# Factorization-machine layer on one core: groups of 1536 columns, outer sums by accumulating DMAs, a 4x2x3 scheme for one of seven inner products

## The chip, the cores and the metric

The kernel runs on one core of a Trainium2 chip. The core has a matrix engine (TensorE, here PE, with its weight loads shown apart as PEld), a vector engine (VectorE, DVE), a scalar engine (ScalarE, ACT), a general engine (GpSimd, POOL) and a queue engine (SyncE, SP) that issues most DMAs. Each engine works through its own instructions in their order and waits on semaphores for the others. The metric is the device time of one execution in microseconds; the median of three runs is 1438.88 us before the change (1438.18 to 1439.22).

## What is computed

```python
out_lin = x @ lin_w.T + lin_b
xv = jnp.einsum('bf,efm->bem', x, weight)
zp = jnp.einsum('bf,efm->bem', jnp.square(x), jnp.square(weight))
interaction = 0.5 * jnp.sum(jnp.square(xv) - zp, axis=1)
return out_lin + interaction
```

x is 1024 x 512, weight 64 x 512 x 512 (embedding e, feature f, model column m), all float32. For every m there are 64 columns of weight, so `xv` is a product of 1024 x 512 with 512 x 32768. Since the second term is summed over e before it is used, it needs only the sums over e of the squared weights (`w2_sum`) and one small product.

## The kernel before

The large product is cut into 16 groups of 32 model columns, 2048 columns each. In each group a fast scheme with seven products (of Strassen's kind) is used twice. The outer one splits x into two halves of rows and two halves of features, and the weight group into quadrants `w11`, `w12`, `w21`, `w22`. Its seven right-hand sides are four quadrants, possibly after a sum in place, and `T1`, `T2`; the sums between quadrants are made by `outer_sum` (L384), eight DVE instructions of 128x1024 a group. Its left-hand sides are sums of blocks of x, kept for all groups in `X1` to `X7`.

Each of the seven outer products is made by `tree` (L416), in the order of `ORDER` (1, 6, 2, 7, 4, 5, 3), again with seven products. `tree` forms four sums `t1` to `t4` on POOL (128x512 each), then runs seven products of two matmuls with 512 columns each (L438). A float32 matmul shows as two MATMUL records with a LDWEIGHTS each, so a group has 196 records. Partial results are shared between products in PSUM: ACT copies a bank to SBUF (`p5`, `p53`) or to another bank (`b2`) at L287 while PE accumulates on; DVE adds banks to `p` or to the outer accumulators `oa`, `ob`, `c` (`outer_psum` L451, `outer_sbuf` L465, all issued at L274); POOL does most adds whose operands both lie in SBUF. When a quadrant of the group's result is complete, `finish` (L402) squares it on ACT (L289) and reduces it over e on DVE (L296) into `acc`. `w_squares` (L394) does the same for the weight quadrants, into `w2_sum`.

At the start the linear part is 32 matmuls (L325) whose result goes to DRAM; at the end 32 matmuls (L565) form the product with `w2_sum`, and the accumulators come back from DRAM.

The order is made when the program is built, by the class `Plan`: every operation has a cost per engine, reads and writes, and `Plan.order` (L62) runs a list schedule. On PE the order is fixed by a key (`7 * s + PLACE[p]`): `pick` takes the next product of the chain or none. The other engines take the operation that is due first among those that are ready. Adds whose operands are in SBUF may go to DVE or POOL. What comes out is one fixed sequence for each engine; nothing is chosen on the chip.

Of the kernel before, what the change touches and what calls it, by code (L numbers as in the profile page):

```python
# [17 lines left out]
G = 2  # L18
ORDER = (1, 6, 2, 7, 4, 5, 3)

SLOT = {1: 0, 7: 1, 2: 2, 4: 3, 5: 4, 6: 5, 3: 6}

PLACE = {5: -6, 3: -2, 1: 0, 6: 3, 2: 4, 7: 6, 4: 9}
# [3 lines left out]
class Plan:  # L27

# [14 lines left out]
    def add(self, costs, emit, reads=(), writes=(), key=None, land=0.0, both=False):  # L43
        op = SimpleNamespace(
            n=len(self.ops), costs=costs, emit=emit, key=key, land=land,
            deps=set(), succ=[], latest=None, end=None, both=both,
        )
        for r in reads:
            if r in self.writer:
                op.deps.add(self.writer[r])  # L50
        for w in writes:
            op.deps.update(self.readers[w])
            if w in self.writer:
                op.deps.add(self.writer[w])
# [4 lines left out]
        op.deps.discard(op.n)  # L59
        self.ops.append(op)  # L60

    def order(self, spare=4.0):  # L62
# [6 lines left out]
        for o in reversed(ops):  # L69
            for d in o.deps:  # L70
                ops[d].succ.append(o.n)
        waiting = [len(o.succ) for o in ops]
        stack = [o for o in ops if not o.succ]
        while stack:
# [3 lines left out]
            for x in o.succ:  # L78
                latest = min(latest, ops[x].latest - cost)
# [11 lines left out]
        done, late, nxt = [], 0.0, 0  # L91
# [5 lines left out]
        def ready(o):  # L97
            return max([0.0] + [ops[d].end for d in o.deps]) + self.HOP
# [35 lines left out]
        while len(done) < len(ops):  # L134
            now = heapq.heappop(times)
            moved = True
            while moved:
                moved = False
                for e in pending:
# [6 lines left out]
                    if e == PE:  # L146
                        nxt += 1
# [25 lines left out]

@with_exitstack
def kernel(
# [8 lines left out]

    nc = tc.nc
    NG, NQ, _, NCB, KH, N = weight.shape
    B = xT.shape[1]
    M = out.shape[1]
    NB = B // P
    NK = 2 * KH
    MG = M // NG
    MI = MG // 4  # L210
    E = N // MI
    H = B // 2
    Q = B // 4

# [9 lines left out]

    buf = {}

    def make(name, shape, pool=sb):
        buf[name] = pool.tile(shape, F32, tag=name, name=name)
        return name

    def ring(tag, n, shape, pool=sb):
        names = [make(f"{tag}_{i}", shape, pool) for i in range(n)]
        state = [0]

        def take():
            state[0] += 1
            return names[(state[0] - 1) % n]
# [3 lines left out]
    half = [P, 2, N]  # L241
    for i in range(1, 8):
        make(f"X{i}", [P, 7, Q])
    for q in ("w11", "w12", "w21", "w22a", "w22b", "T1", "T2"):
        for c in range(NCB):
            make(f"{q}.{c}", half)
    for pos in range(4):
        make(f"oa{pos}", half)
        make(f"ob{pos}", half)
    t_ring = {k: ring(f"t{k}", 2, [P, N]) for k in range(1, 5)}  # L250
    p5_ring, p53_ring = ring("p5", 2, half), ring("p53", 3, half)
    c_ring, wsq_ring = ring("c", 3, half), ring("wsq", 2, half)
    make("b1", [P, G, N], ps)
    make("b3", [P, G, N], ps)
    b2_ring = ring("b2", 2, [P, G, N], ps)
    acc_ring = ring("acc", 2, [P, NB, MG])
    w2_sum = sb.tile([P, NK, M], F32, tag="w2_sum", name="w2_sum")
    bias = sb.tile([P, M], F32, tag="bias", name="bias_sb")
# [5 lines left out]
    PAIR = 1.72  # L264

    def two_input(o, a, b, sub, size=1024, psum=False):

        costs = {DVE: 0.08 + 1.06 * size / 1024}
        if not psum:
            costs[POOL] = 0.14 + 2.19 * size / 1024  # L270

        def emit(e):
            f = engines[e].tensor_sub if sub else engines[e].tensor_add
            f(o, a, b)  # L274

        return costs, emit

    def whole(o, a, b, sub=False, only=None, psum=False):

        costs, emit = two_input(buf[o], buf[a], buf[b], sub, psum=psum)  # L280
        plan.add({e: c for e, c in costs.items() if only in (None, e)}, emit, (a, b), (o,),
                 both=not psum)

    def act(o, i, func, reads, writes, cost=1.04):
        def emit(_):
            if func is None:
                nc.scalar.copy(o, i)  # L287
            else:
                nc.scalar.activation(o, i, func)  # L289

        plan.add({ACT: cost}, emit, reads, writes)

    def reduce(o, i, reads, writes):
        plan.add(
            {DVE: 1.14},
            lambda _: nc.vector.tensor_reduce(  # L296
                o, i.rearrange("p a (m e) -> p a m e", e=E), axis=AX.X, op=ALU.add
            ),
            reads, writes,
        )  # L300
# [3 lines left out]


    x_src = xT.rearrange("(p k) b -> p k b", k=NK)
    lw_src = lin_wT.rearrange("(p k) m -> p k m", k=NK)
    nc.gpsimd.dma_start(bias, lin_b.partition_broadcast(P))
    for k in range(NK):
        q, r = divmod(k, KH)  # L310
        for h in range(2):
            name = f"oa{2 * h + q}"
            dma(buf[name][:, r, :], x_src[:, k, ts(h, H)], (), ((name, r),),
                1.2, 2.0, nc.sync if h == 0 else nc.scalar)
        dma(buf[f"ob{q}"][:, r, :], lw_src[:, k, :], (), ((f"ob{q}", r),), 1.2, 2.0)

    lin_banks = ["b1", "b3", "b2_0", "b2_1"]
    for k in range(NK):
        q, r = divmod(k, KH)
        for g, bank in enumerate(lin_banks):  # L320
            h = g // 2

            def emit(_, k=k, q=q, r=r, g=g, h=h, bank=bank):
                for j in range(G):
                    nc.tensor.matmul(  # L325
                        buf[bank][:, j, :],
                        buf[f"oa{2 * h + q}"][:, r, ts((g * G + j) % (NB // 2), P)],
                        buf[f"ob{q}"][:, r, :],
                        start=(k == 0),
                        stop=(k == NK - 1),  # L330
                    )

            plan.add({PE: PAIR}, emit, ((f"oa{2 * h + q}", r), (f"ob{q}", r)),
                     (bank,), key=-1000 + 4 * k + g)
    for g, bank in enumerate(lin_banks):
        o = ("ob2", "ob3", "c_0", "c_1")[g]
        for j in range(G):
            costs, emit = two_input(buf[o][:, j, :], buf[bank][:, j, :], bias, False, 512, True)
            plan.add(costs, emit, (bank,), ((o, j),))
        dma(lin_dram[:, ts(g, G), :], buf[o], ((o, 0), (o, 1)), (o,))  # L340

    def block4(i):
        return buf[f"X{i}"][:, 0:4, :].rearrange("p (k q) b -> p k (q b)", k=2)

    a_buf = {"A11": "oa0", "A12": "oa1", "A21": "oa2", "A22": "oa3"}

    def a_parts(*names):
        return tuple((a_buf[n], r) for n in names if n in a_buf for r in range(KH)) + tuple(
            n for n in names if n not in a_buf
        )  # L350

    def a_ap(n):
        return buf[a_buf[n]] if n in a_buf else block4(int(n[1]))

    for i, n in ((1, "A11"), (2, "A12"), (4, "A22")):
        act(block4(i), a_ap(n), None, a_parts(n), (f"X{i}",))
    for i, a, b, sub in ((5, "A21", "A22", 0), (6, "X5", "A11", 1), (7, "A11", "A21", 1), (3, "A12", "X6", 1)):
        costs, emit = two_input(block4(i), a_ap(a), a_ap(b), sub)
        plan.add(costs, emit, a_parts(a, b), (f"X{i}",), both=True)
    for i in ORDER:  # L360
        x = buf[f"X{i}"]
        a11, a21, a12, a22 = (x[:, s, :] for s in range(4))
        s1, s2, s4 = (x[:, s, :] for s in range(4, 7))
        for o, a, b, sub in ((s1, a21, a22, 0), (s2, s1, a11, 1), (s4, a12, s2, 1), (a21, a11, a21, 1)):
            costs, emit = two_input(o, a, b, sub, 256)
            plan.add(costs, emit, (f"X{i}",), (f"X{i}",), both=True)
    for n in a_buf.values():
        plan.add({SP: 0.0}, None, (), (n,) + tuple((n, r) for r in range(KH)))
    for n in ("ob0", "ob1", "ob2", "ob3", "c_0", "c_1"):
        plan.add({SP: 0.0}, None, (), (n, (n, 0), (n, 1)))  # L370


    QUAD = ("w11", "w12", "w21", "w22")

    def w(g, q):
        return q + "ab"[g % 2] if q == "w22" else q

    def load(g):
        for q in (0, 1, 3, 2):
            for c in range(NCB):  # L380
                n = f"{w(g, QUAD[q])}.{c}"
                dma(buf[n], weight[g, q][:, c], (), (n,))

    def outer_sum(g, which):  # L384
        o, a, b = {
            1: ("T1", "w12", "w11"),
            2: ("T2", w(g, "w22"), "T1"),
            3: ("w12", w(g, "w22"), "w12"),
            4: ("w21", "w21", "T2"),
        }[which]  # L390
        for c in range(NCB):
            whole(f"{o}.{c}", f"{a}.{c}", f"{b}.{c}", True, DVE)

    def w_squares(g, q):  # L394
        row, col = divmod(QUAD.index(q), 2)
        for c in range(NCB):
            n, sq = f"{w(g, q)}.{c}", wsq_ring()
            act(buf[sq], buf[n], AF.Square, (n,), (sq,), 1.07)
            m = g * MG + (2 * col + c) * MI
            reduce(w2_sum[:, ts(row, KH), m:m + MI], buf[sq], (sq,), (("w2", row, m),))  # L400

    def finish(g, i, n, pos):  # L402
# [211 lines left out]
```

## Time and profile before

| | us |
|---|---|
| median of the runs | 1438.88 |
| span of the profiled execution, first to last instruction | 1436.8 |
| PE busy | 1408.8 |
| DVE busy | 1245.7 |
| POOL busy | 1149.6 |
| ACT busy | 748.8 |

The runs' times hold a little more than the span, which begins with the first instruction and ends with the last. Busy times add up an engine's instructions; matmuls are pipelined and their records overlap, so the pitch from one to the next says more than their length. In a group's row stand line, engine, operation, result and operands by the program's names, shape and count, then busy time in us and the mean of one in ns, then the idle time just before it and what ended it. The granted clock of TensorE is 1.000 on average.

### The profile page before, as it was taken

How to read it: one execution, taken by the hardware profiler on the slowest of the kernel's cores; microseconds unless marked ns; L12 is line 12 of the kernel's file. 1: busy time of each engine (PE TensorE's matmuls, PEld its weight loads, DVE VectorE, ACT ScalarE, POOL GpSimd, SP SyncE). 2: the span in 40 equal slices, each digit the busy share in tenths (PEclk: the TensorE clock that was granted, in tenths of full speed). 3: DMA queues.
4: the chain of work that ended last, by engine and by line, in shares of the span. 5: the costliest groups of instructions: out<-in, count | busy, mean ns of one | idle time of the engine just before them, and what ended most of it. 6: DMA issues, size and time to landing. Idle time of an engine off the chain costs nothing.

```text
span 1436.8 us, 10763 instructions
## 1 busy us (share of the span) xinstructions
PE 1408.8 (98%) x3264; PEld 619.3 (43%) x3264; DVE 1245.7 (87%) x1006; ACT 748.8 (52%) x756; POOL 1149.6 (80%) x691
## 2 busy tenths in 40 slices
PE   7999999999999999999999999999999999999998
PEld 3444444444444444444444444444444444444443
DVE  1899898998989899898988989899898888989984
ACT  1465554645545465564556555465554546556441
POOL 6988886878878688896878888687887868889781
PEclk9999999999999999999999999999999999999999
DMA  5311111111111112111111111111111111210221
GB/s 212 117 60 58 48 59 33 59 48 59 59 42 51 33 59 62 46 58 33 59 48 58 59 48 59 33 59 48 58 59 45 53 32 57 60 52 22 88 74 59
DMA packets 40377, 83.54 MB, mean 58 GB/s; under 512 B 18240, under 2 KB 19264, under 8 KB 40320
## 3 DMA queue, kind: packets, MB, share of 16 engines
q1 hardware_dynamic: 39664, 81.54, 18.1%
q10 hardware_dynamic: 576, 1.05, 0.2%
q8 instruction: 27, 0.44, 0.1%
q14 instruction: 30, 0.25, 0.1%
q0 software_dynamic: 80, 0.26, 0.0%
HBM read 76.68 MB, written 6.16 MB: 58 GB/s over the span
## 4 chain that ended last, share of the span: by engine, by line
PE 90%; POOL 4%; DVE 2%; issue 1%; ACT 1%; DMA 1%; DVEq 0%; POOLq 0%; SPq 0%
PE b L438 86%; POOL oa L274 3%; PE b L325 2%; PE b L565 2%; ACT p L287 1%; POOL t L274 1%; DMA ob<-lin_wT 0%; DVE p L274 0%; DMA T1.1_83<-lind 0%; DVE ob L274 0%; DVE w11.1_73 L536 0%; DVE w21.0_76 L274 0%; DVE oa L274 0%; DVE acc L296 0%; DVE w11.0_72 L536 0%
## 5 line engine op out<-in xcount | busy, mean ns | idle before, releaser
L438 PE MATMUL b<-t,X 128*128 128x512 f32 x1792 | 806.2, 592 | 2.0 <-DVE p L274 1.6
L438 PEld LDWEIGHTS b<-t,X 128*128 128x128 f32 x1792 | 340.0, 190 | 431.9 <-issue 415.0
L287 ACT COPY p<-b 128x1024 f32<-128x1024 f32 x224 | 225.6, 1007 | 266.1 <-PE b L438 226.8
L289 ACT ACTIVATE oa<-oa 128x1024 f32<-128x1024 f32 x128 | 131.9, 1054 | 165.3 <-DVE oa L274 90.9
L296 DVE TENSOR_REDUCE w_sum<-wsq 128x16 f32<-128x1024 f32 x128 | 154.8, 1211 | 29.0 <-ACT wsq L289 28.9
L287 ACT COPY b<-b 128x1024 f32<-128x1024 f32 x112 | 111.8, 998 | 91.1 <-PE b L438 85.2
L274 DVE TENSOR_TENSOR p<-b,p 128x1024 f32<-128x1024 f32 x96 | 117.0, 1218 | 43.4 <-PE b L438 43.4
L296 DVE TENSOR_REDUCE acc<-oa 128x16 f32<-128x1024 f32 x128 | 152.0, 1207 | 0.0
L438 PE MATMUL b<-w21.0_76,X 128*128 128x512 f32 x256 | 120.3, 592 | 0.0
L274 POOL TENSOR_TENSOR oa<-oa,p 128x1024 f32<-128x1024 f32 x32 | 102.8, 3212 | 1.8
L289 ACT ACTIVATE c<-c 128x1024 f32<-128x1024 f32 x64 | 67.7, 1058 | 67.8 <-DVE c L274 67.8
L274 POOL TENSOR_TENSOR oa<-p,oa 128x1024 f32<-128x1024 f32 x32 | 75.7, 2365 | 27.2 <-DVE p L274 26.9
L274 DVE TENSOR_TENSOR oa<-b,p 128x1024 f32<-128x1024 f32 x64 | 78.0, 1219 | 11.7 <-PE b L438 10.8
L274 POOL TENSOR_TENSOR c<-c,oa 128x1024 f32<-128x1024 f32 x32 | 75.4, 2357 | 13.8 <-DVE c L274 11.7
L274 POOL TENSOR_TENSOR oa<-oa,ob 128x1024 f32<-128x1024 f32 x32 | 76.4, 2387 | 6.9 <-DVE oa L274 6.9
L274 POOL TENSOR_TENSOR ob<-ob,oa 128x1024 f32<-128x1024 f32 x32 | 76.3, 2384 | 5.5 <-DVE ob L274 5.5
L274 POOL TENSOR_TENSOR t<-w21.0_76,t 128x512 f32<-128x512 f32 x32 | 40.8, 1275 | 48.3 <-PE b L438 48.3
L274 POOL TENSOR_TENSOR ob<-p,ob 128x1024 f32<-128x1024 f32 x32 | 75.7, 2364 | 0.5 <-DVE p L274 0.5
L296 DVE TENSOR_REDUCE acc<-ob 128x16 f32<-128x1024 f32 x64 | 75.9, 1209 | 0.0
L296 DVE TENSOR_REDUCE acc<-c 128x16 f32<-128x1024 f32 x64 | 74.8, 1208 | 1.1 <-ACT c L289 1.1
L438 PEld LDWEIGHTS b<-w21.0_76,X 128*128 128x128 f32 x256 | 48.6, 190 | 61.2 <-issue 61.2
L274 DVE TENSOR_TENSOR ob<-b,oa 128x1024 f32<-128x1024 f32 x32 | 39.1, 1223 | 40.5 <-PE b L438 39.8
(127 smaller groups left out, 2295.9 us busy)
## 6 DMA issues: line engine op xcount, KB each, us to landing
w11.0_72<-weight SPq DMA_DIRECT2D x16, 512.0 KB, 3.7
w11.1_73<-weight SPq DMA_DIRECT2D x16, 512.0 KB, 3.8
w12.0_74<-weight SPq DMA_DIRECT2D x16, 512.0 KB, 3.8
w12.1_75<-weight SPq DMA_DIRECT2D x16, 512.0 KB, 3.8
w21.0_76<-weight SPq DMA_DIRECT2D x16, 512.0 KB, 3.8
w21.1_77<-weight SPq DMA_DIRECT2D x16, 512.0 KB, 4.7
w22a.0_78<-weight SPq DMA_DIRECT2D x8, 512.0 KB, 3.8
w22a.1_79<-weight SPq DMA_DIRECT2D x8, 512.0 KB, 3.8
```

The lines of the kernel that those rows point to most:

```text
L274: f(o, a, b)
L287: nc.scalar.copy(o, i)
L289: nc.scalar.activation(o, i, func)
L296: lambda _: nc.vector.tensor_reduce(o, i.rearrange("p a (m e) -> p a m e", e=E), axis=AX.X, op=ALU.add),
L325: nc.tensor.matmul(buf[bank][:, j, :], buf[f"oa{2 * h + q}"][:, r, ts((g * G + j) % (NB // 2), P)], buf[f"ob{q}"][:, r, :], start=(k == 0) ...
L438: nc.tensor.matmul(buf[b][:, j, :], buf[f"X{i}"][:, SLOT[p], ts(j, P)], op, start=first, stop=True, skip_group_check=True,)
L565: nc.tensor.matmul(buf[bank][:, j, :], buf[xe[h, k // KH]][:, k % KH, ts((g * G + j) % (NB // 2), P)], w2_sum[:, k, :], start=(k == 0), st ...
```

## The change

The groups become two of 16 model columns (1024 columns) and then twenty of 24 (1536 columns). Matmuls have 256 columns in the first two groups and 384 in the others.

`outer_sum` no longer runs on DVE: `T1` and `T2` are loaded from DRAM as copies of `w12` and `w22`, and the four sums of a group are DMAs that add to their destination, issued from POOL's queue. Signs in the x blocks are changed so that all four are additions. `T1` gets a second buffer.

On PE, `Plan.order` takes, among the products that are ready and due within 20 us, the one with the lowest key. Dependencies are kept by regions (`Reg`) of one large tile for each name instead of by tile, and two-row tiles become strided regions. The rings of `p53` and of the sums `t` are shorter.

Outer product 1 of each wide group is made by `wide_tree`: four row blocks by two feature blocks by three column blocks with 20 products of one 256-column matmul each, where `tree` has 14 matmuls of 384. It needs eight sums on POOL, and more PSUM copies on ACT. `widen` turns `X1` into the 20 left-hand sides, once.

```diff
-G = 2
+HK = (1,)
+HSEQ = (17, 10, 0, 19, 7, 4, 6, 3, 14, 16, 9, 1, 18, 11, 12, 8, 2, 15, 5, 13)
+TBUF = 3
+SPARE = 4.0
+AHEAD = 20.0
...
+def groups(n_m):
+    return [16, 16] + [24] * ((n_m - 32) // 24)
...
             if e == PE:
-                if nxt < len(chain):
-                    o = chain[nxt]
-                    if not left[o.n] and ready(o) <= now + 1e-6:
-                        return o
-                return None
+                able = [n for n in pending[e]
+                        if ops[n].latest < now - late + AHEAD and ready(ops[n]) <= now + 1e-6]
+                return ops[min(able, key=lambda n: ops[n].key)] if able else None
...
+    def dma_add(o, i, rows, reads, writes):
+        token = ("token", len(plan.ops))
+
+        def emit(_):
+            nc.gpsimd.dma_start(o, i, accum_op=ALU.add)
+
+        cost = 2.9 * rows / 1024
+        plan.add({POOL: 1.0}, emit, reads + writes, writes + (token,), land=cost + 2.5)
+        plan.add({SP: cost}, None, (token,), ())
...
     def outer_sum(g, which):
-        o, a, b = {
-            1: ("T1", "w12", "w11"),
-            2: ("T2", w(g, "w22"), "T1"),
-            3: ("w12", w(g, "w22"), "w12"),
-            4: ("w21", "w21", "T2"),
-        }[which]
-        for c in range(NCB):
-            whole(f"{o}.{c}", f"{a}.{c}", f"{b}.{c}", True, DVE)
+        o, i = {
+            1: (w(g, "T1"), None), 2: ("T2", w(g, "T1")), 3: ("w12", w(g, "w22")), 4: ("w21", "T2"),
+        }[which]
+        n = KH * GROUPS[g] // 2 * E
+        o = reg(o, 0, n)
+        if i is None:
+            dma_add(o.ap, source(g, 0), n, (), o.atoms)
+        else:
+            dma_add(o.ap, reg(i, 0, n).ap, n, reg(i, 0, n).atoms, o.atoms)
...
+    def wide_tree(time, g, i, fresh_bank):
...
+        sums = (
+            (t(9), bk(0, 1), bk(1, 1), 0),
+            (t(0, 2), cols(0), twice(bk(0, 1)), 1),
+            (t(2, 2), t(0, 2), twice(bk(1, 1)), 1),
+            (t(4, 2), t(2, 2), cols(1), 0),
+            (t(11), bk(1, 0), bk(1, 2), 0),
+            (t(8), t(11), bk(1, 1), 1),
+            (t(6, 2), t(0, 2), twice(t(8)), 0),
+            (t(10), t(6), bk(0, 0), 0),
+        )
+        for o, a, b, sub in sums:
+            tt(o, a, b, sub, POOL)
...
+        def product(p, b, half, first=False):
+            mm([h(b, half)], [reg(f"X{i}", HSLOT[p] * P, P)], rhs[p], first,
+               time + (HSEQ.index(p) - HLEAD) * cost)
...
+        product(17, "U", 0, True)
+        copy(Reg(h("Q").tile, h("Q").off, V, (V, 2)), twice(h("U", 0)))
+        product(10, "T", 1, True)
+        product(0, "T", 0)
+        copy(h("S"), h("T"))
+        copy(pp, h("T"))
...
+        product(13, "S", 0)
+        leave("S", 0, (0, 1), n5, extra_sub=True)
...
+    for g, mg in enumerate(GROUPS):
         acc_name[g] = acc_ring()
-        load(g)
+        load(g, (("w11", 0), ("w12", 1), (w(g, "T1"), 1), ("T2", 3)))
         outer_sum(g, 1)
         outer_sum(g, 2)
+        load(g, ((w(g, "w22"), 3), ("w21", 2)))
...
+            hk = i in HK and mg == max(GROUPS)
+            if hk and GROUPS[g - 1] != mg:
+                widen(i)
```

More of the change, by code (lines that the diff above doesn't have):

```diff
@@ L236, in take @@
             state[0] += 1
-            return names[(state[0] - 1) % n]
+            return names[(state[0] - 1) % len(names)]
         return take
-    half = [P, 2, N]
     for i in range(1, 8):
-        make(f"X{i}", [P, 7, Q])
-    for q in ("w11", "w12", "w21", "w22a", "w22b", "T1", "T2"):
-        for c in range(NCB):
[L246 to L258, printed above, removed]
+        make(f"X{i}", 20 * P if i in HK else 7 * Q)
+    for q in ("w11", "w12", "w21", "w22a", "w22b", "T1a", "T1b", "T2"):
+        make(q, KH * WIDE)
+    make("oa", 4 * WIDE)
+    make("ob", 4 * WIDE)
+    make("c", 4 * WIDE)
+    t_ring = ring([make(f"t{k}", 12 * V) for k in range(TBUF)])
+    p5_ring = ring([make(f"p5_{k}", WIDE) for k in range(2)])
+    p53_ring = ring([make(f"p53_{k}", WIDE) for k in range(2)])
+    wsq_ring = ring([make(f"wsq{k}", WIDE) for k in range(2)])
+    for name in ("b1", "b3", "b2_0", "b2_1"):
+        make(name, 2 * N, ps, N)
+    b2_ring = ring(["b2_0", "b2_1"])
+    acc_ring = ring([make(f"acc{k}", NB * max(GROUPS), sb, 4) for k in range(2)])
+    make("w2_sum", NK * M, sb, 4)
+    make("bias", M)
     acc_dram = dram.tile([P, NB, M], F32, tag="accd", name="accd")
@@ L272, in emit @@
         def emit(e):
             f = engines[e].tensor_sub if sub else engines[e].tensor_add
[L274 to L284, printed above, removed]
+            f(o.ap, a.ap, b.ap)
+        plan.add({e: c for e, c in costs.items() if only in (None, e)}, emit,
+                 a.atoms + b.atoms, o.atoms, both=not psum)
@@ L285, in emit, with copy @@
+    def copy(o, i, negative=False):
         def emit(_):
-            if func is None:
-                nc.scalar.copy(o, i)
-            else:
[L289 to L300, printed above, removed]
+            if negative:
+                nc.scalar.activation(o.ap, i.ap, AF.Copy, scale=-1.0)
+            else:
+                nc.scalar.copy(o.ap, i.ap)
+        plan.add({ACT: 0.19 + 0.00083 * o.size}, emit, i.atoms, o.atoms)
@@ L337 @@
[L337 to L349, printed above, removed]
-        )
@@ L352, in a_ap @@
[L352 to L359, printed above, removed]
+        name, off = ("c", g * 2 * M) if g < 3 else ("w22b", 0)
@@ new lines, with x_block, minus_both @@
+        for j in range(2):
+            tt(reg(name, off + j * M, M), reg(bank, j * N, N), reg("bias"))
+        o = reg(name, off, 2 * M)
+        dma(lin_dram[:, ts(g, 2), :].rearrange("p a m -> p (a m)"), o.ap, o.atoms, (("lin", g),))
+    def x_block(i):
+        return reg(f"X{i}", 0, 4 * Q)
+    for i, a in ((1, (0, 0)), (2, (0, 1)), (4, (1, 1))):
+        copy(x_block(i), x_in(*a))
+    def minus_both(o, a, b):
+        plan.add(
+            {DVE: 0.08 + 1.06 * o.size / 1024},
+            lambda _: nc.vector.scalar_tensor_tensor(
+                o.ap, a.ap, -1.0, b.ap, ALU.mult, ALU.subtract
+            ),
+            a.atoms + b.atoms, o.atoms, both=True,
+        )
@@ L550 @@
[L550 to L555 removed]
+            {DVE: 0.15 + 1.09 * 2 * (hi - lo) / 1024},
+            lambda _: nc.vector.scalar_tensor_tensor(
+                view(r, lo, hi), a, 0.5, view(r, lo, hi), ALU.mult, ALU.add
+            ),
```

508 lines of the change are left out of this document (341 added, 167 removed).

## The prediction

> **What bounds the kernel now.** I read first the busy shares on the page, then the chain of work that ended last in order of time.
>
> ```profile
> span 1436.8 us, 10763 instructions
> PE 1408.8 (98%) x3264; PEld 619.3 (43%) x3264; DVE 1245.7 (87%) x1006; ACT 748.8 (52%) x756; POOL 1149.6 (80%) x691
> ```
> ```profile
> 1.19 6.57 DMA ob<-lin_wT
> 7.90 30.40 PE b L325 x64
> ...
> 1225.26 3.30 POOL oa L274
> 1230.59 79.25 PE b L438 x184
> 1310.46 3.30 POOL oa L274
> ...
> 1404.63 27.48 PE b L565 x64
> ```
>
> PE is the bound: its weight of 98% is no artefact of long records, because the last 64 matmul records (32 matmuls, two records each) follow each other without a gap in 27.48 us, 0.42938 us each. At that pitch 3264 records take 1401.5 us. The other 35.3 us of the span are: 7.9 before the first matmul; 30.40 - 27.48 = 2.9 because the first records ran slower; 4.7 behind the last matmul (1436.8 - 1404.63 - 27.48); and about 20 of waits.
>
> ```profile
> PE b L438 <- ACT p L287: 13.4, 16, 1.1
> ```
>
> A group comes every 85.2 us (1310.46 - 1225.26); its 196 records at 0.42938 need 84.16, so 1.04 us is lost at each group border, 16 times by the list of waits. The timeline there shows how (start, duration, engine, line, operation; in brackets the idle time and its releaser):
>
> ```profile
> 714.02 3.33 POOL L274 TENSOR_TENSOR oa<-oa,p 128x1024 f32<-128x1024 f32 x1
> 717.30 2.25 POOL L274 TENSOR_TENSOR t<-w21.1_77,w21.0_76 128x512 f32<-128x512 f32 x1
> 719.52 1.27 POOL L274 TENSOR_TENSOR t<-w11.0_72,t 128x512 f32<-128x512 f32 x1
> 720.75 1.27 POOL L274 TENSOR_TENSOR t<-T2.1_85,T2.0_84 128x512 f32<-128x512 f32 x1
> 721.98 2.38 POOL L274 TENSOR_TENSOR ob<-p,ob 128x1024 f32<-128x1024 f32 x1
> 724.30 1.29 POOL L274 TENSOR_TENSOR t<-T2.1_85,t 128x512 f32<-128x512 f32 x1
> ```
> ```profile
> 717.38 1.06 ACT L289 ACTIVATE oa<-oa 128x1024 f32<-128x1024 f32 x1 [4.64 <-POOL oa L274]
> 718.34 0.99 ACT L287 COPY p<-b 128x1024 f32<-128x1024 f32 x1
> ```
> ```profile
> 715.06 3.36 DVE L274 TENSOR_TENSOR T2.0_84<-w22a.0_78,T1.0_82 128x1024 f32<-128x1024 f32 x1
> 718.35 1.21 DVE L274 TENSOR_TENSOR p<-b,p 128x1024 f32<-128x1024 f32 x1
> ```
>
> ```profile
> 716.68 1.88 PE L438 MATMUL b<-w22b.0_80,X 128*128 128x512 f32 x4
> 719.39 1.98 PE L438 MATMUL b<-w11.1_73,X 128*128 128x512 f32 x4 [0.82 <-ACT p L287]
> ```
>
> POOL's add takes 3.33 us beside a DVE outer sum that reads two SBUF tiles (3.36), against 2.38 for the same size a few adds later; the next, of 512, takes 2.25 against 1.27. ACT's square waits for that add, ACT's copy of a PSUM bank stands behind the square in ACT's queue, and PE waits for the copy: its four records from 716.68 are over at 718.40, the next start at 719.39. So the border stall is a late POOL, passed on through ACT.
>
> **PE's work after.** From the program's order I count 3360 records of 384 columns, 1192 of 256 and 128 of 512. By columns alone they cost 3360 x 0.32204 + 1192 x 0.21469 + 128 x 0.42938 = 1392.9 us, 8.6 less than before; that is the 20-product scheme (5120 columns a group instead of 5376). Against it stand 1416 more records.
>
> ```profile
> 8.88 0.34 PEld L325 LDWEIGHTS b<-ob,oa 128*128 128x128 f32 x1 [0.52 <-issue]
> ...
> 13.15 0.28 PEld L325 LDWEIGHTS b<-ob,oa 128*128 128x128 f32 x1 [0.52 <-issue]
> 13.67 0.19 PEld L325 LDWEIGHTS b<-ob,oa 128*128 128x128 f32 x1 [0.24 <-issue]
> ```
>
> A fixed part per record can be read from the start, where the same records ran at half speed. Five steps from 8.88 to 13.15 are 0.854 each. If streaming halves exactly and a fixed part is hidden in the slow state, streaming is 0.427 and the fixed part 0.0024. Then the records cost 0.3227, 0.2159 and 0.4294, together 1396.5 us: 5.0 less than before. I take this; its bounds are 1392.9 (no fixed part) and 1400 (twice as much).
>
> ```profile
> 709.61 0.40 PEld L438 LDWEIGHTS b<-w22b.0_80,X 128*128 128x128 f32 x2 [0.46 <-DVE ob L274]
> 710.25 0.19 PEld L438 LDWEIGHTS b<-w22b.0_80,X 128*128 128x128 f32 x1 [0.24 <-issue]
> ```
>
> A 256-column record must still cover the next weight load, 0.19 us; the cover left is 0.026, and two loads have stood back to back in 0.40, so a pitch of 0.20 is possible. If a load did stick out, each 0.01 us would cost 1192 x 0.01 = 12 us.
>
> A wide group so has 168 x 0.3227 + 40 x 0.2159 = 62.8 us of PE. Everything else must fit in that.
>
> **DVE and ACT.** DVE loses its outer sums, 128 + 15 instructions that read two SBUF tiles, and so the partner of POOL's 3.3 us adds; in the built order DVE has no such instruction in the middle groups. A wide group leaves it 50 instructions of 768 elements and 4 of 256.
>
> ```profile
> 1386.08 1.13 DVE c L274
> 1387.21 1.13 DVE acc L296
> ```
> ```profile
> L274 DVE TENSOR_TENSOR p<-b,p 128x1024 f32<-128x1024 f32 x96 | 117.0, 1218 | 43.4 <-PE b L438 43.4
> L274 DVE TENSOR_TENSOR ob<-b,bias_sb 128x512 f32<-128x512 f32 x4 | 2.6, 681 | 12.2 <-PE b L325 12.2
> L289 ACT ACTIVATE c<-c 128x1024 f32<-128x1024 f32 x64 | 67.7, 1058 | 67.8 <-DVE c L274 67.8
> ```
>
> From 1.13 us from start to start at 1024 and the difference to a 512 one, 0.86 at 768 and 0.33 at 256. That is 44.3 of 62.8 us (71%, before 87%). ACT has 51 instructions a group, most of them shorter than before; at the full price of a 1024 one, 1.06, they make 54. Neither becomes the bound.
>
> **POOL is the tight one.** POOL's starts in the border rows are 1.23 apart behind a 512 add and 2.32 behind a 1024 one (721.98 to 724.30): 0.14 + 2.13 ns per element, so 0.685 at 256, 0.958 at 384, 1.775 at 768. A wide group gives it 24 of 384, 14 of 768, 4 of 512, 4 of 256 and four DMA issues: 23.0 + 24.9 + 4.9 + 2.7 = 55.5 us and four issues. Slack is 7.3 us less the issues.
>
> ```profile
> L308 POOL DMA_DIRECT2D bias_sb<-lin_b x1 | 0.7, 677 | 0.8 <-POOLq L603 0.8
> ```
> ```profile
> w11.0_72<-weight SPq DMA_DIRECT2D x16, 512.0 KB, 3.7
> w21.1_77<-weight SPq DMA_DIRECT2D x16, 512.0 KB, 4.7
> bias_sb<-lin_b POOLq DMA_DIRECT2D x1, 256.0 KB, 7.4
> ```
>
> The only DMA on POOL's queue so far is the bias. Its issue took 0.677 us for rows of 2 KB; the new rows are 6 KB. Bounds for one issue: 0.68 and 3 x 0.68 = 2.03; I take 1.0, nearer the lower end since both have 128 rows. POOL then has 59.5 of 62.8 us, 95%, where it had 80% before. From 1.83 us an issue on, POOL and not PE sets the group.
>
> What stands behind the DMAs on POOL matters as much, for POOL goes in order. In the built order the sum into w21 is followed by 2 adds of 768 and 3 of 384 until the first add that reads it (6.4 us of work); T2 by 7.9 us; w12 by 10.2; T1 by 24 instructions. A landing later than that stops all of POOL, and with it ACT's squares and PE as at the border. Bounds for the landing of 768 KB: 3.7 (a 512 KB load, nothing dearer) and 14.1 (4.7 x 1.5 for the bytes, twice because the destination is read too). I take 7, the slow load scaled by its bytes: 0.6 us of waiting a group, inside the slack of 3.3. The Trainium skill, DMA: Bandwidth & Descriptors, section Anatomy of one DMA — SWDGE (gpsimd) path, fits 2.0 us plus bytes at 436 GB/s for a DMA issued from GpSimd, an estimated 3.8 us here; by it POOL never waits, the sum stays and the chance of the slower rival below goes to the forecast. No run here shows an accumulating DMA, and the page does not say that its fit holds for one.
>
> ```profile
> q1 hardware_dynamic: 39664, 81.54, 18.1%
> ```
>
> SP, whose queue carries the loads, issues 12 a group instead of 8. The DMA engines were 18% busy and get, counting an accumulation double, 14 quarter passes over the weights for 4, so at most 63%. Loads are a group ahead, so I cost them at nothing; without that cover they lengthen the landing, which is in its range.
>
> **Stalls after.** The 16.7 us at the borders (16 times 1.04) rest on a locked POOL add; that goes.
>
> ```profile
> 1357.62 5.42 PE L438 MATMUL b<-t,X 128*128 128x512 f32 x12 [0.37 <-POOL t L274]
> 1394.14 3.67 PE L438 MATMUL b<-t,X 128*128 128x512 f32 x8 [0.20 <-DVE p L274]
> 1402.68 1.96 PE L438 MATMUL b<-t,X 128*128 128x512 f32 x4 [1.44 <-DVE p L274]
> ```
>
> The waits near the end (0.37, 0.20 and 1.44 us) I leave as they are in kind, about 2 us.
>
> New ones: taking matmuls as they become ready only changes a fixed order, on the chip PE still stops at the first one that is not; a POOL at 95% leaves perhaps 0.2 us a wide group, 4 us, bounds 0 and 1.04.
>
> ```profile
> 11.76 1.52 POOL L274 TENSOR_TENSOR X<-X 128x256 f32<-128x256 f32 x2 [9.84 <-ACT X L287]
> ```
>
> At the start POOL gets all 28 sums of 256 on X (25 before): 19.2 us, with 4.6 for two whole blocks, 19.2 and 17.2 for the first group's adds and 4 for its issues, 64 us. POOL can begin at 11.7 and is done at 76, PE with the first narrow group at 7.9 + 30.4 + 196 x 0.2159 = 80.6: hidden, by 5 us. The widening of X1 is 12 short adds on POOL, about 6 us in all, spread up to the second narrow group; if they find no slack they cost 6 us once.
>
> Sum: 1396.5 + 7.9 + 2.9 + 4.7 + 2 + 4 = 1418 span. Executions run about 2 us over the span (median 1438.88 against 1436.8), so **1420 us**.
>
> **The rivals.**
> - No new stall at all and no fixed part: 1392.9 + 15.5 + 2.1 = 1410. For it: DVE's relief; against it: POOL's 95%.
> - The stall only moves. The 4x2x3 tree has longer chains of PSUM copies with half-bank products; if PE loses 1.04 us in each of 20 groups, 1396.5 + 15.5 + 2 + 20.8 + 2 = 1437, the same as before. Here the change would not do what it says. For it: the border stalls passed through ACT, whose queue is as in-order as ever; against it: the order puts neighbouring trees' products between the tree's steps.
> - POOL's issue is dear: at 2.03 us POOL has 63.6 a group, 0.8 over PE: 16 us more than forecast less the 4 already in, 1432. For: three times the bytes; against: the same number of rows.
> - Slower: accumulating DMAs land late and POOL stands in front of the first reader. A landing of L costs (L - 6.4) + (L - 7.9) a group, less 3.3 of slack, 20 times; it eats the forecast's 19 us from L = 9.3 on, and at L = 10 it is 48 us: 1468. For: the 7.4 us of the bias with a third of the bytes, though it ran beside the first loads; against: 3.7 for plain loads.
>
> **How the numbers follow.** Chances: forecast 0.55, none lost 0.08, stall moves 0.09, dear issue 0.10, late landing 0.18. A difference within 0.2% (2.9 us, about what a measurement of this kernel can tell from none) counts as the same. Faster are the forecast, the case without stalls, the dear issue and 0.04 of the moved stall, together 0.77; the other 0.05 of the moved stall is the same; the late landing is slower, 0.18. The range reaches from 1409, just under the case without stalls, to 1446, some way into the late landings: about 0.15 is left above and 0.02 below it. The forecast's own range is 1411 to 1430.
>
> **What would show it.** In the profile after: 384-column records 0.32 apart and 256 ones 0.216 (right) or more (the load sticks out); no add on POOL longer than 1.9 us at 768; POOL busy near 90 to 95%; POOL idle less than 2 us a group in front of reads of w21, T2 or w12 (right) or more than 4 (the slower rival); groups 62.8 to 63.2 us apart. Wrong would be groups of 64 us and more.

## The result and the profile after

The changed kernel takes 1485.08 us (median of three runs, 1483.65 to 1488.68) against 1438.88: ratio 1.0327, 95% interval 1.0313 to 1.0341. It is slower; the forecast of 1420 and its range up to 1446 missed. The profiled execution's own time is 1488.68 us.

The busy shares of the page after:

```profile
span 1486.9 us, 15088 instructions
PE 1425.1 (96%) x4680; PEld 883.4 (59%) x4680; DVE 1058.4 (71%) x1255; ACT 806.8 (54%) x1158; POOL 1296.5 (87%) x1139
```

PE fell from 98 to 96%, and no other engine took its place. What PE's work itself costs is seen in its timeline (start, duration, operation, count):

```profile
50.61 1.89 PE L335 MATMUL b<-t,X 128*128 128x256 f32 x8
52.34 1.89 PE L335 MATMUL b<-T,X 128*128 128x256 f32 x8
...
736.63 1.45 PE L335 MATMUL b<-T,X 128*128 128x384 f32 x4
737.92 1.45 PE L335 MATMUL b<-t,X 128*128 128x384 f32 x4
```

Eight records of 256 columns take 1.73 us, 0.216 each; four of 384 take 1.29, 0.3225 each. At 0.2159, 0.3226 and 0.4294 us for records of 256, 384 and 512 columns the 4680 records cost 1396.3 us. The time that was lost is between the records. The chain of waits shows one wide group and the next:

```profile
689.85 42.52 PE b L335 x134
...
732.45 0.58 ACT b L299
...
733.07 8.90 PE b L335 x34
...
742.00 0.70 DVE oa L289
...
742.78 0.38 ACT oa L299
...
743.18 0.44 DVE oa L289
...
743.64 0.78 ACT b L299
744.42 1.00 ACT p L299 x2
...
745.47 52.04 PE b L335 x164
...
798.21 8.90 PE b L335 x34
...
810.60 19.54 PE b L335 x61
```

The same place returns after 810.60 - 745.47 = 65.13 us, where PE has 62.8 us of work: 2.3 us are lost in each wide group. They are lost at two places, both inside `wide_tree`, and the list of PE's waits puts them down to ACT's copies of PSUM banks, once each in 19 groups; the wait for `c` and several for `oa` belong to the start:

```profile
PE b L335 <- ACT p L299: 16.9, 19, 0.9
PE b L335 <- ACT b L299: 13.6, 19, 0.7
PE b L335 <- DVE c L289: 7.0, 1, 7.0
PE b L335 <- DVE oa L289: 6.7, 8, 3.4
```

`wide_tree` calls the six PSUM banks that it uses Q to V; a bank is 512 float32 columns of PSUM, the memory that matmuls write to. The first stall stands in front of product 7, which writes bank Q; the copy it waits for writes bank S from T. Product 7 touches neither S nor T. The second stands in front of product 5, again in Q; it waits for the copy `n5` out of S, and that copy (the second of the two in the last row below; the row's shape is the first one's) stands in ACT's queue behind copies for other trees, one of which waits for DVE. Here is that queue, and an add of DVE beside it:

```profile
742.78 0.37 ACT L299 COPY oa<-b 128x256 f32<-128x256 f32 x1 [2.57 <-DVE oa L289]
743.64 0.78 ACT L299 COPY b<-b 128x768 f32<-128x768 f32 x1 [0.49 <-DVE oa L289]
744.34 1.08 ACT L299 COPY p<-b 128x768 f32<-128x768 f32 x2
```
```profile
742.00 0.69 DVE L289 TENSOR_TENSOR oa<-b,p 128x512 f32<-128x512 f32 x1 [0.98 <-PE b L335]
```

Q and S are two banks of one tile (`b2_0` or `b2_1`, two banks each). The planner of the changed kernel counts what touches a tile by bank (`make(name, 2 * N, ps, N)`). In the built program the wait goes by tile, so far as these rows tell: an instruction on one bank waits for the last one on the other bank too. The first row of ACT shows it where both only read: that copy reads V, and it waits 2.57 us until DVE's add, which reads R, is over; R and V are two banks of one tile. So the planner put product 7 right behind the copy, thinking that it was free to run. Before the change the planner counted by whole tiles too, and the two countings agreed. The runs below test this.

The gaps can be added up over the whole trace: from the start of one matmul record to the next, less 0.2159, 0.3226 or 0.4294 by its columns (records at half clock count with their excess). That gives 34.0 us from 0 to 300 us, 37.8 from 300 to 1340 (16 groups of 2.3) and 7.3 after; before the change it was 7.3, 12.5 and 2.7. The start is the second loss, though not all of another kind: the first wide group begins before 145 us, and its tree's stalls and those of the next are in the 34.0. DVE and POOL there:

```profile
34.12 7.74 DVE L391 SCALAR_TENSOR_TENSOR X<-oa,X 128x1024 f32<-128x1024 f32 x1
41.78 2.47 DVE L289 TENSOR_TENSOR c<-b,bias 128x512 f32<-128x512 f32 x4
```
```profile
34.34 1.03 POOL L289 TENSOR_TENSOR X<-X 128x256 f32<-128x256 f32 x1
35.02 1.02 POOL L289 TENSOR_TENSOR t<-w 128x256 f32<-128x256 f32 x1
...
39.80 0.97 POOL L289 TENSOR_TENSOR t<-w,t 128x256 f32<-128x256 f32 x1
41.94 0.73 POOL L289 TENSOR_TENSOR X<-X 128x256 f32<-128x256 f32 x1 [1.17 <-DVE X L391]
```
```profile
43.20 2.04 PE L335 MATMUL b<-t,X 128*128 128x256 f32 x4 [7.03 <-DVE c L289]
```

`minus_both`, with two SBUF inputs on DVE, lasts 7.74 us: POOL's adds go on beside it at 0.68 us from start to start, and it ends 1.1 us after the last of them is over (40.77 to 41.86). The bias adds of the linear part stand behind it in DVE's queue, and PE waits 7.03 us for their banks.

### The profile page after: what moved, and what is told of

Read it like the earlier page. It is cut to its first block, busy times and chain, and to the rows that moved or that the text cites. A ratio compares the mean times of both kernels' runs of the same rounds, so it can differ in the third digit from the quotient of the medians.

```text
span 1486.9 us, 15088 instructions
## 1 busy us (share of the span) xinstructions
PE 1425.1 (96%) x4680; PEld 883.4 (59%) x4680; DVE 1058.4 (71%) x1255; ACT 806.8 (54%) x1158; POOL 1296.5 (87%) x1139
## 4 chain that ended last, share of the span: by engine, by line
PE 87%; ACT 4%; DVE 3%; DMA 2%; issue 1%; POOL 0%; DVEq 0%; ACTq 0%; SPq 0%
PE b L335 86%; DVE oa L289 2%; ACT b L299 2%; PE b L776 2%; ACT p L299 1%; DMA w<-weight 1%; DMA w<-T 1%; DVE acc L314 0%; ACT oa L299 0%; DVE p L289 0%; DMA T1b<-lind 0%; DMA X<-xT 0%; DVE X L744 0%; DVE T1b L758 0%; ACT wsq L305 0%
## 5 line engine op out<-in xcount | busy, mean ns | idle before, releaser
L335 PE MATMUL b<-t,X 128*128 128x384 f32 (+1 forms) x2584 | 832.1, 464 | 45.3 <-ACT p L299 16.2
L335 PEld LDWEIGHTS b<-t,X 128*128 128x128 f32 x2584 | 484.0, 191 | 347.5 <-ACT p L299 28.3
L335 PE MATMUL b<-w,X 128*128 128x384 f32 (+1 forms) x1176 | 369.1, 447 | 4.9 <-DVE oa L289 4.2
L299 ACT COPY p<-b 128x768 f32<-128x768 f32 (+1 forms) x328 | 230.3, 714 | 215.6 <-PE b L335 215.3
L335 PEld LDWEIGHTS b<-w,X 128*128 128x128 f32 x1176 | 224.5, 191 | 123.6 <-ACT p L299 5.7
L289 POOL TENSOR_TENSOR t<-w 128x384 f32<-128x384 f32 (+2 forms) x196 | 198.1, 1028 | 78.4 <-PE b L335 65.5
L305 ACT ACTIVATE oa<-oa 128x768 f32<-128x768 f32 (+1 forms) x176 | 142.5, 822 | 177.3 <-DVE oa L289 135.8
L314 DVE TENSOR_REDUCE w_sum<-wsq 128x12 f32<-128x768 f32 (+1 forms) x176 | 160.5, 923 | 66.1 <-ACT wsq L305 65.9
L314 DVE TENSOR_REDUCE acc<-oa 128x12 f32<-128x768 f32 (+1 forms) x176 | 157.3, 921 | 9.6 <-ACT oa L305 9.5
L289 POOL TENSOR_TENSOR t<-w,t 128x384 f32<-128x384 f32 (+1 forms) x136 | 138.8, 1021 | 4.3 <-PE b L335 2.9
```

What stands on the lines that cost most here:

```text
L289: f(o.ap, a.ap, b.ap)
L299: nc.scalar.copy(o.ap, i.ap)
L305: lambda _: nc.scalar.activation(o.ap, i.ap, AF.Square), i.atoms, o.atoms)
L314: nc.vector.tensor_reduce(o, x, axis=AX.X, op=ALU.add)
L335: nc.tensor.matmul(a.ap, b.ap, w.ap, start=start, stop=True, skip_group_check=True)
```

## The experiments

All medians are beside runs of the kernel before on the same chip (1438.4 to 1438.7; 1438.9 for the first row). "Group" is the mean time from one wide group to the next, "gaps" are PE's as above, from 0 to 300 and from 300 to 1340 us. Both are read from one profiled execution, which for e5 and e10 was the fastest of ten (1438.9 and 1432.1 us).

| kernel | median, us | ratio to before (95%) | group, us | gaps 0-300 | gaps 300-1340 |
|---|---|---|---|---|---|
| after | 1485.1 | 1.0327 (1.0313-1.0341) | 65.1 | 34.0 | 37.8 |
| e1_no_wide | 1458.8 | 1.0140 (1.0125-1.0155) | 64.1 | 22.1 | 15.0 |
| e2_tile_deps | 1497.0 | 1.0412 (1.0396-1.0427) | 66.0 | 29.5 | 49.3 |
| e3_split_two | 1508.0 | 1.0487 (1.0471-1.0502) | 66.3 | 37.3 | 53.9 |
| e4_split_one | 1429.1 | 0.9940 (0.9923-0.9957) | 62.9 | 16.9 | 1.3 |
| e5_start | 1443.2 | 1.0029 (1.0020-1.0039) | 62.9 | 27.1 | 1.2 |
| e6_one_no_wide | 1434.2 | 0.9970 (0.9958-0.9982) | 63.2 | 15.6 | 0 |
| e7_dve_sums | 1514.7 | 1.0530 (1.0496-1.0564) | 67.3 | 28.1 | 69.2 |
| e8_strict | 1585.5 | 1.1017 (1.0999-1.1036) | 70.4 | 43.0 | 111.3 |
| e9_pool_only | 1440.7 | 1.0015 (1.0004-1.0026) | 63.5 | 17.9 | 11.1 |
| e10_pool_adds | 1435.2 | 0.9974 (0.9965-0.9984) | 63.4 | 12.0 | 9.2 |
| e11_strict_no_wide | 1568.6 | 1.0901 (1.0885-1.0917) | 69.4 | 38.2 | 91.9 |
| e12_load_land | 1422.8 | 0.9887 (0.9871-0.9904) | 62.8 | 12.1 | 0.1 |

### The 4x2x3 tree taken out

```diff
-HK = (1,)
+HK = ()
```

> Outer product 1 is made by the 7-product tree in every group, all else of the change stays. Its 28 records of 384 columns cost 0.40 us a group more than 40 of 256. Theory (the 4x2x3 tree's products wait for copies of the other bank of their PSUM tile, 2.3 us a wide group): groups 63.3 to 63.8 us apart instead of 65.1, no PE wait of 0.7 us or more on an ACT copy in the steady groups, time 1448 to 1460. Rival (POOL sets the pace): POOL loses 3.8 us a group, so it would give the same time here; the next two runs tell them apart. Rival (the reordered matmuls or the accumulating DMAs cost it): groups stay 65 apart, time 1485 to 1495.

1458.8 us, in the expected range, and the two waits on ACT copies are gone; but groups are 64.1 apart, not 63.3 to 63.8. PE has 63.2 us of work in them, so 0.9 is still lost without the tree. The tree is not the whole of the loss.

### The planner told of whole tiles

```diff
-        make(name, 2 * N, ps, N)
+        make(name, 2 * N, ps, 2 * N)
```

> The planner counts what touches a PSUM tile by the whole tile of two banks, as the waits in the built program do, instead of by bank. Same instructions, other order. Theory: the planner then sees the waits and puts other products ahead of them; the stalls of the 4x2x3 tree shrink but its chain of copies is longer for it, groups 63.3 to 64.5 us apart, time 1450 to 1470. Rival (POOL sets the pace) and rival (accumulating DMAs): POOL's work and the DMAs are the same, groups stay 65 apart, 1480 to 1490.

A miss: 1497.0, slower still. The planner that knows the waits does not get round them:

```profile
PE b L335 <- ACT b L299: 16.9, 19, 2.1
PE b L335 <- DVE p L289: 11.0, 44, 2.1
```

The wait for ACT is as frequent as before and longer, and waits for DVE's adds join it. Either the waits by tile are not the cause, or no order that this planner finds gets round them; that is told apart by taking their ground away.

### Each bank a tile of its own

To have one tile for each bank, instructions that cover two banks have to be cut in two. That alone is the control (e3); e4 has the same instructions and one-bank tiles.

```diff
-        def whole(bank):
-            return reg(bank, 0, n, (N, 2))
+        def half(bank, j):
+            return bank_reg(bank, j * N, n)
...
-                copy(part("oa", pos), whole(bank))
+                for j in range(2):
+                    copy(ph("oa", pos, j), half(bank, j))
...
-        make(name, 2 * N, ps, N)
+        for j in range(2):
+            make(f"{name}.{j}", N, ps, N)
```

(the last hunk in e4 alone)

> Control for the next run: every DVE and ACT instruction that covers both banks of a PSUM tile is cut in two, one for each bank; tiles and planner stay. About 30 short instructions a group more on DVE (some 0.08 us each) and 18 on ACT (0.19 each). All theories: the stalls of the 4x2x3 tree stay or grow, groups 65 to 66.5 us apart, time 1483 to 1515.

> As the control, with each PSUM bank a tile of its own, so that the built waits go by bank as the planner counts. Theory: the two stalls a wide group (0.9 and 1.1 us) go, groups 62.9 to 63.5 us apart, time 1440 to 1455, 30 to 60 us under the control. Rival (POOL sets the pace) and rival (accumulating DMAs, reordered matmuls): within 5 us of the control.

The control took 1508.0, as expected; with one-bank tiles it is 1429.1, 79 us less and 9 us under the kernel before. That is more than the theory's 30 to 60 us: the gaps of the start fall too, from 37.3 to 16.9. In the two traces PE, ACT, DVE and POOL each run the same instructions in the same order, so only the waits differ. The rows of the windows view for 300 to 1340 us (length; PE, PEld, DVE, ACT, POOL busy with counts; clock, DMA share, GB/s), first the changed kernel, then the control, then one-bank tiles:

```profile
300.00:1340.00 1040.00, 1013.26 (x3320) 623.20 (x3319) 763.01 (x895) 598.96 (x847) 942.90 (x798) 1.00 0.52 123
```
```profile
300.00:1340.00 1040.00, 1012.05 (x3261) 606.30 (x3259) 771.74 (x1291) 615.00 (x1114) 930.48 (x785) 1.00 0.50 121
```
```profile
300.00:1340.00 1040.00, 1040.00 (x3444) 652.30 (x3443) 823.74 (x1363) 647.82 (x1179) 979.30 (x827) 1.00 0.53 125
```

With one-bank tiles PE is busy in all of 1040 us and gets through 3444 records instead of 3320; at 208 a group that is 62.8 us each. POOL is busy for 979 of 1040 us (94%), and the list of PE's waits is empty in this stretch: POOL does not set the pace. The accumulating DMAs and the order by readiness are all still there. The waits by tile were the loss of the middle groups: the gaps there fall from 53.9 to 1.3 us.

### What each part is worth without those waits

> Each bank its own tile, and outer product 1 by the 7-product tree in every group. PE gets 20 times 0.40 us more work. Theory (with waits by bank the 4x2x3 tree costs nothing but its matmuls, and is worth its 0.40 us a group): 1435 to 1440, groups 63.2 apart. Rival (its copies and adds still cost about what its fewer columns bring): 1426 to 1431.

e6 is e4 without the 4x2x3 tree: 1434.2, groups 63.2 apart with no gap at all. The tree brings 5.1 us; the time lies just under the theory's range, and above the rival's. With the 1.3 us that e6 loses less at the start and 1.3 in the middle it is 7.7, near 20 times 0.40. The 0.9 us a group that e1 still lost is gone with one-bank tiles.

```diff
-            dma_add(o.ap, reg(i, 0, n).ap, n, reg(i, 0, n).atoms, o.atoms)
+        tt(o, o, reg(i or "w11", 0, n), False, DVE)
```

> Each bank its own tile, and the four sums of a group as DVE additions of 128x1536 (two SBUF inputs, about 1.7 us each) in place of the accumulating DMAs. Theory (the DMAs were no part of the loss, and they free POOL from DVE's two-input reads): PE waits come back where a POOL add runs beside such a sum, 0.5 to 2 us a group, 1438 to 1470. Rival (the DMAs cost as much as they bring): 1424 to 1432.

e7 makes the outer sums on DVE: 1514.7, far outside what either theory gave. Groups of POOL in the middle stretch show why (busy time, mean ns):

```profile
L294 POOL TENSOR_TENSOR c<-c,oa 128x768 f32<-128x768 f32 x32 | 58.5, 1828 | 0.0
L294 POOL TENSOR_TENSOR oa<-p,oa 128x768 f32<-128x768 f32 x16 | 53.4, 3335 | 0.0
```

Once a group a POOL add of 768 takes 3.34 us instead of 1.83 beside a DVE sum, and PE waits for POOL's sums again, 1.6 us in each of 16 groups; not all of the 69.2 us of gaps is traced to that. With DVE sums in place of the DMAs 86 us come back. The DMAs were no part of the loss of the middle groups, since e4 has them too.

```diff
-                return ops[min(able, key=lambda n: ops[n].key)] if able else None
+                o = chain[nxt[0]] if nxt[0] < len(chain) else None
+                if o is None or left[o.n] or ready(o) > now + 1e-6:
+                    return None
+                nxt[0] += 1
+                return o
```

> Each bank its own tile, and PE's order by key alone, as before the change, instead of what becomes ready. Theory (the reordering only changes a fixed order and is worth little): 1425 to 1440. Rival (the reordering is what hides the 4x2x3 tree's chain of copies): every tree stops PE for a copy or two, 1.5 us or more a group, 1460 and more.

> Each bank its own tile, PE's order by key alone, and the 7-product tree in every group. It tells what the reordering hides: if it hides only the 4x2x3 tree's chain of copies, 1434 to 1450; if it also hides the landing of the accumulating DMAs (6 us, in front of POOL's sums for products 7 and 4), 3 to 7 us a group stay, 1490 to 1580.

With PE's order by key alone e4 takes 1585.5, and without the 4x2x3 tree still 1568.6. The theory of e8 is far off, and e11 lies in the range of its second case: the order by readiness does not hide the tree's copies only. POOL and then PE of e8, at one place of a group:

```profile
735.98 0.87 POOL L332 DMA_DIRECT2D w<-T  x1 [0.44 <-PE b1.1_93 L342]
...
742.05 1.95 POOL L296 TENSOR_TENSOR t<-w 128x384 f32<-128x384 f32 x2 [0.65 <-DMA w<-T]
```
```profile
743.09 1.65 PE L342 MATMUL b3.0_94<-t,X 128*128 128x384 f32 x2 [3.55 <-POOL t L296]
```

The DMA that adds `T2` to `w21` can start only when outer product 2 has read `w21` for the last time, and lands 6 us later; only outer product 7 lies between 2 and 4 in `ORDER`. In the fixed order PE runs out of work; in the order by readiness it takes products of other trees meanwhile.

### The start

```diff
-    minus_both(x_block(6), x_block(5), x_in(0, 0))
+    copy(x_block(6), x_block(5), True)
+    tt(x_block(6), x_block(6), x_in(0, 0), True, POOL)
...
-    minus_both(x_block(3), x_in(0, 1), x_block(6))
+    copy(x_block(3), x_in(0, 1), True)
+    tt(x_block(3), x_block(3), x_block(6), True, POOL)
```

> Each bank its own tile, as in e4_split_one; and at the start X6 and X3 no longer come from two DVE instructions that read two SBUF tiles (4.43 and 7.73 us there beside POOL's adds, with the linear part's bias adds behind them in DVE's queue) but from a negating copy on ACT and a subtraction on POOL (2.3 us each). Theory (the start lost its time to those two DVE instructions): the bias adds run when the linear matmuls end, PE's 4.7 us wait for them goes, and with it some slow matmuls after it; time 1417 to 1424 against 1429. Rival (POOL's own work at the start sets the end of the first groups): POOL is 4.6 us later, the wait moves to POOL's sums, 1427 to 1434.

A miss. PE's wait of 4.7 us is gone, but 1443.2 is 14 us slower than e4. Two other instructions with two SBUF inputs, which the planner now gave to DVE, met POOL's adds:

```profile
80.54 7.33 DVE L294 TENSOR_TENSOR oa<-oa,p 128x512 f32<-128x512 f32 x1 [0.45 <-POOL c L294]
...
142.83 10.24 DVE L294 TENSOR_TENSOR oa<-oa,p 128x512 f32<-128x512 f32 x1
```

PE waited 6.2 and 8.2 us for them. So I bound all such adds to POOL, with (e9) and without (e10) the edit of e5:

```diff
-        costs = {DVE: 0.08 + 1.06 * o.size / 1024}
-        if not psum:
-            costs[POOL] = 0.14 + 2.19 * o.size / 1024
+        if psum or only == DVE:
+            costs = {DVE: 0.08 + 1.06 * o.size / 1024}
+        else:
+            costs = {POOL: 0.14 + 2.19 * o.size / 1024}
```

> As e5_start, and every addition whose operands both lie in SBUF is bound to POOL, so DVE has no instruction with two SBUF inputs beside POOL's adds (in e5_start two such 128x512 adds of DVE took 7.33 and 10.24 us, and PE waited 6.2 and 8.2 us for them). Theory (at the start the loss is each time such a DVE instruction, wherever the planner puts it): no PE wait over 3 us between 30 and 300 us, time 1417 to 1425. Rival (POOL has too much to do in the first 150 us, whoever holds it up): the waits stay and end on POOL's sums, 1430 to 1440.

> As e4_split_one, with every two-SBUF addition but the two of X6 and X3 bound to POOL. Theory: the two long DVE instructions at 28 and 34 us stay and with them PE's 4.7 us wait; else nothing is late: 1425 to 1431, some 5 us over e9_pool_only. Rival (POOL overloaded at the start): over 1431.

Both miss, at 1440.7 and 1435.2. The second lies where its rival had it, the first just over its rival's 1440. No wait over 3 us is left between 30 and 300 us in e9, as the theory wanted, but the gaps of the start are 17.9 us in many pieces. In e10 they are 12.0, five less than in e4: of the two long DVE instructions that were to stay, the second took 1.45 us there instead of 7.73, while one of POOL's adds of 256 beside it took 1.72 instead of 0.73, and PE's wait of 4.7 us was gone:

```profile
33.29 1.45 DVE L398 SCALAR_TENSOR_TENSOR X<-oa,X 128x1024 f32<-128x1024 f32 x1
```

What e10 wins at the start is lost in the middle groups: with the planner's choice gone the gaps there are 9 to 11 us in both kernels. That the start is simply too full, so that a wait taken away at one place comes back at another, is not shown: it fits e9, not e10.

The next suspect came from the chain of waits of e4:

```profile
104.66 5.40 DMA w<-weight
110.14 0.85 ACT wsq L310
111.01 0.95 DVE w_sum L319
111.97 0.66 DVE oa L294 x2
...
114.20 0.70 PE b_0.0_96 L340 x2
```

A weight load lands in 5.4 us, and a square and its reduction, whose result is needed only at the end, stand in ACT's and DVE's queues in front of work that PE waits for: the planner counted with an earlier landing.

```diff
-                dma(o.ap, source(g, q)[:, k * iw:(k + 1) * iw], (), o.atoms, 2.4 * iw / 1024)
+                dma(o.ap, source(g, q)[:, k * iw:(k + 1) * iw], (), o.atoms, 2.4 * iw / 1024, 5.0)
```

> As e4_split_one, with the planner told that a weight load lands 5.0 us after its queue time instead of 1.5. In e4_split_one loads of w took 5.4 and 6.6 us at 105 and 166 us, with a square on ACT or its reduction on DVE put ahead of work that PE waited for. Theory (those waits at the start come from squares placed too early): PE's waits of 0.9 to 1.8 us between 100 and 180 us go, 1423 to 1428. Rival (the start is full, the wait comes back elsewhere): 1428 to 1434.

1422.8, a little below the theory's range: 6 us less than e4 and 16 under the kernel before, the fastest of all. Its gaps are 12.1 us at the start and 0.1 from 300 to 1340. The theory names most of the gain, but not all: from 100 to 300 us the gaps fall from 6.5 to 2.7, and only one PE wait, of 0.47 us, is left between 100 and 180. The new order also moved the start itself. Six of the eight bias adds now run ahead of the second long DVE instruction, the wait of 4.7 us is gone, one of 2.7 has come in its place, and the gaps before 60 us fall from 9.5 to 6.8; those from 60 to 100 us grow from 0.9 to 2.7. Which of the waits at the start are left for which reason was not tried further.

## Why the prediction was wrong, by its steps

- **PE's work: right.** 1396.5 forecast, 1396.3 by the measured pitches; no weight load sticks out.
- **DVE, ACT: right that neither bounds.** In the middle stretch DVE is busy 47.8 us a wide group, against 44.3 forecast, and ACT 37.5, against 54 as an upper figure. That DVE's share of the span came out at the forecast's 71% is luck: both the work and the span are longer.
- **POOL: right, with one bad sign.** It is busy 59 us a wide group, against 59.5 forecast. Its adds of 768 start 1.78 us apart; the records themselves are about 2.0 us long since they overlap, so "no add longer than 1.9" was a poor thing to look for. An issue of an accumulating DMA takes 0.78 to 1.12 us in the middle groups (taken: 1.0), and the landings are near the 7 taken:

```profile
w<-T POOLq DMA_DIRECT2D x20, 768.0 KB, 6.0
T1a<-weight POOLq DMA_DIRECT2D x10, 768.0 KB, 7.7
T<-T1a POOLq DMA_DIRECT2D x10, 768.0 KB, 6.2
w<-w22a POOLq DMA_DIRECT2D x10, 768.0 KB, 8.5
```

  The rivals of a dear issue and of a late landing both fell: POOL in the changed kernel waits 94.3 us for PE in all and 4.2 for the DMA into `w21`.
- **"Stalls after", 0.2 us a wide group: the step that failed.** It was 2.3. I gave the bounds 0 to 1.04 from the old border stall, which has another cause. The rival "the stall only moves" named the place (the 4x2x3 tree, copies of PSUM banks, half-bank products) but borrowed the same price, and the reason I gave against it, that neighbouring trees' products stand between the tree's steps, was the planner's picture, not the built program's. The gap between the two, bank against tile, could be read before any run, in the waits of the built program; I did not look there. So the step had the wait itself wrong, not only its size: it costed a late POOL, and PE stopped for copies in banks that its next product did not touch. One-bank tiles (e4) show that the step would have been right with waits by bank: 62.9 us a group.
- **The start, "hidden, by 5 us": failed too.** I summed POOL's work as if it ran without disturbance and nothing stood behind it. The gaps up to 300 us were 34.0, with 2.9 forecast. About half goes with one-bank tiles (16.9 in e4), 5 more with a longer landing time of the loads in the planner (12.1 in e12). So "loads are a group ahead, so I cost them at nothing" holds for the middle groups; at the start the planner's figure for them changed the order, and with it the time. The causes of the 12.1 us that are left stay open.
- **"Taking matmuls as they become ready only changes a fixed order": true, and costed as if the order were worth nothing.** Without it e4 loses 156 us. It did not enter the sum, since the order that I read was already the new one.
- **The sum.** 1418 forecast; plus 31 at the start, plus 34.5 in the middle (37.8 against 3.3), plus 4.6 after 1340 us (7.3 against 2 and 0.7), less about 1 at the two ends: 1487, the span measured. e12, which keeps every part of the change, came within 3 us of the forecast time, with one-bank tiles and split instructions that the forecast did not have.

## What to carry to other kernels

Where a planner outside the compiler decides the order, compare what it takes for a dependency with the waits that the build makes: here a tile of two PSUM banks was one thing to the waits, however finely the planner counted. Give each bank that is used by itself its own tile, before judging a scheme that works on halves. And price a stall by the chain at its new place, not by the stall that the change removes.

## What the runs showed of the hardware

- A DVE instruction with two SBUF inputs did not take turns with POOL. In e5 a 128x512 one, 0.68 us when its other input is in PSUM, took 10.24 us, while POOL's adds kept their pitch; the 128x1024 one at 34.12 us in the changed kernel was not over before the nine POOL adds begun after it were. The Trainium skill, SBUF — State Buffer, section Who interferes with whom, says that a DVE instruction with two SBUF inputs contends with a GpSimd instruction that reads SBUF, and that issue order decides who blocks. The contention agrees. But the loser here waited for a whole train of instructions, and the instruction at 34.12 had begun 0.22 us before the first of the nine adds by the trace, whose spans on POOL are rough. It can go the other way: in e7 POOL's add took 3.34 us instead of 1.83, and in e10 the DVE instruction that takes 7.73 us in e4 took 1.45.
- A long PE wait is followed by half speed, and so are some shorter ones. The windows view of e8 before its wait of 3.55 us and right behind it, and of the changed kernel behind a wait of 2.11 us that ends at 1417.85 (with the row of that wait):

```profile
735.00:739.00 4.00, 4.00 (x14) 2.34 (x13) 2.23 (x4) 1.87 (x4) 3.56 (x4) 1.00 0.50 98
743.00:746.40 3.40, 3.31 (x5) 1.83 (x6) 1.53 (x3) 2.04 (x4) 2.94 (x4) 0.50 0.78 234
```
```profile
1417.85 4.54 PE L335 MATMUL b<-t,X 128*128 128x384 f32 x8 [2.11 <-DVE p L289]
```
```profile
1418.80:1422.10 3.30, 3.30 (x6) 1.69 (x5) 1.67 (x2) 1.69 (x2) 1.95 (x2) 0.50 0.25 70
```

  In e8 the clock was 0.50 there, and 1.00 again by 749 us by the records' pitch. The waits of 0.7 to 0.9 us in the middle groups of the changed kernel left it at 1.00. The Trainium skill, TensorE: Matmul & The Clock Gate, section What's actually happening, gives an idle window of about 3.4 us as the point. The 3.55 us agree with that, but 2.11 us here and 2.66 us in e12 (0.50 from 44.8 to 48.1 us) were enough, and 3.11 us in e6 were not (1.00 from 114.5 to 118): the length of a wait alone did not decide it. What does is not shown. So lost time can cost more in one long piece than in several short ones.
- An accumulating DMA of 768 KB landed 6.0 to 8.5 us after its issue, a plain load of 384 KB in 3.1 to 4.2 (medians by tile in the changed kernel); a load took 5.4 at the start of e4. The prediction's estimate of 3.8 us for an accumulating DMA was too low.
